# Layer 0's gate product on GpSimd instead of VectorE, in a four-layer graph network

## The chip, the cores and the metric

The kernel runs on one core of a Trainium2 chip. The metric is the device time of one execution in microseconds (us). Time before: the median of three runs is 3009.3 us (3008.72 to 3012.13).

The engines are named as in the profile: PE (TensorE, matmuls and transposes; PEld is its weight load), DVE (VectorE), ACT (ScalarE), POOL (GpSimd) and SP (SyncE, which here only starts DMAs). Each engine works off its own queue in order, and waits on semaphores for the others.

## The reference

Sixteen graphs (`B`) of 1024 nodes (`N`) with 128 features go through four layers, each followed by `x = layernorm(x + layer(x))`. Only layer 0 matters here, a gated attention over the adjacency matrix:

```python
h = x @ W_w.T + W_b
e = jnp.einsum('bjl,bkl->bjk', h @ A, h)
e = e + jnp.swapaxes(e, 1, 2)
att = jnp.where(adj > 0, e, -9e15)
att = jax.nn.softmax(att, axis=1) * adj
h_prime = jax.nn.relu(jnp.einsum('bij,bjk->bik', att, h))
coeff = jax.nn.sigmoid(jnp.concatenate([x, h_prime], axis=-1) @ gate_w.T + gate_b)
return coeff * x + (1.0 - coeff) * h_prime
...
x = _layernorm(x + _L0_gnn_ref(x, adj, ...), axis=-1)
```

`coeff` is one number for each node. With the residual, the sum to be normed is `(1 + coeff) * x + (1 - coeff) * h_prime`. The kernel takes the sigmoid from a tanh, so that `1 + coeff` is `0.5 * tanh + 1.5` (tile `cx`) and `1 - coeff` is `-0.5 * tanh + 0.5` (tile `co`).

Layer 1 is a graph convolution on a thinned adjacency matrix; a stage of its own does the thinning between layers 0 and 1. Layers 2 and 3 need a power of the nodes' degrees, among other things.

## The kernel before

`fast_kernel` does the work; `general_kernel` is a second path that runs only if a flag is set at the end, and it plays no part here. Nodes lie on 128 partitions in 8 tiles (`NT`), so that a graph's features are a tile of 128 x 8 x 128.

Layer 0 is written as three generators for a graph `b`, each cut into steps by `yield`:

- `before` loads x into `s.xn` (L916) and then, in eight steps, one block of 128 adjacency rows `an` (L920). ACT turns it into bf16 with the row sums (L922), DVE tests its values (L925, tile `chk`), PE transposes it (L929), and DVE writes the transposed 0/1 block as fp8 into `carry` (L930). In between come x transposed (L934), h (L938), the x part of the gate (L941), G (L945) and h in rows (L949). At the end POOL starts the write of the adjacency to DRAM (L951).
- `attention` does one column block in each of eight steps: the mask on ACT (L962), e on PE (helper line L723, tile `pmm`), the masked maximum on DVE (L965, which writes `em`), its negative (L967), the exponential on ACT (L969), reciprocal and scaled h on DVE (L971, L973), and the product on PE into `acc` (L976). There are two `em` buffers.
- `after` has three steps. The first takes relu (L982, tile `hpT`), the gate on PE (L774, L779), and `cx` and `co` on DVE (L985, L989, L990, with a tanh on ACT, L987). The second multiplies x by `cx` (L993), turns h' back with PE transposes (L758) and multiplies each half by `co` out of PSUM into `r` (L995, twice), then adds (L996). The third is the layernorm (`normed`: statistics L793 and L795, the power -1/2 on POOL L741 and L744, L798, and the scaling on ACT L800), and the write of the result, started by POOL (L999).

`in_turn` (L814) interleaves them: while graph b is in `attention`, graph b-1 is in `after` and graph b+1 in `before`, and each turn takes one step of each, in the order after, attention, before. For the last graph, `attention` runs with a step of `after` of graph 14 at every second step, and then `after` of graph 15 runs alone.

This written order is only a priority. When the kernel is built, each engine's queue gets its order from what counts as ready, so instructions of several steps, and of the stage that follows, stand between each other. The semaphores are set then too.

POOL does little in layer 0: for each graph the power in L744, and the start of the two writes L951 and L999. Once, POOL takes the power -1/2 of all 128 columns of degrees (L1177), after DVE has prepared them (L1176). These two lines are written after layer 0, in the thinning stage, and need only the row sums of all graphs.

Of the kernel before, what the change touches and what calls it, by code (L numbers as in the profile page):

```python
# [17 lines left out]
OP = mybir.AluOpType  # L18
# [621 lines left out]
def fast_kernel(ctx: ExitStack, tc: tile.TileContext, t: dict, out: bass.AP, flag: bass.AP):  # L640

    nc = tc.nc
# [43 lines left out]
    def nat(ap):  # L686
        return ap.rearrange("(t p) d -> p t d", p=P)
# [39 lines left out]
    def tiles3(ap):  # L727
        return ap.rearrange("p (t d) -> p t d", d=P)

    def per_row(v):  # L730

        return v[:, :, None].to_broadcast([P, NT, P])
# [20 lines left out]
    def turned(psum, src, tag="h"):  # L753

        for p, c, blocks in halves(psum, tag):
            for i, k in enumerate(blocks):
                s = src[:, k, :] if len(src.shape) == 3 else src[:, k * P:(k + 1) * P]
                nc.tensor.transpose(p[:, i * P:(i + 1) * P], s, identf)  # L758
            yield p, c, slice(blocks[0], blocks[-1] + 1)
# [8 lines left out]
    def gates(psum, out, *pairs):  # L768


        p = psum.tile([P, N // 4], F32, name="pq", tag="h")
        for i, (g, x) in enumerate(pairs):
            for q in range(4):
                nc.tensor.matmul(p[32 * q:32 * q + 32, :], g, x[:, q * N // 4:(q + 1) * N // 4], start=(i == 0),  # L774
                                 stop=(i == len(pairs) - 1), tile_position=(0, 32 * q))
        nc.scalar.copy(out, p)
        p = psum.tile([P, 2, P], F32, name="pg", tag="h")
        for t in range(2):
            nc.tensor.transpose(p[:, t, :], out[:, t * P:(t + 1) * P], identf)  # L779
        return p.rearrange("p t (q g) -> p q t g", q=4)  # L780

    def half_rows(v):

        return v[:, :, None].to_broadcast([P, 4, P])

    def normed(small, r, fine=False):

        for k in spans(fine):
            n = k.stop - k.start
            st = small.tile([P, NT, 6], F32, name="ln_st")  # L790
            mv = small.tile([P, NT, 2], F32, name="ln_mv")
            for i in range(n):
                nc.vector.bn_stats(st[:, i, :], r[:, k.start + i, :])  # L793
            for i in range(n):
                nc.vector.bn_aggr(mv[:, i, :], st[:, i, :])  # L795
            rstd = power_mhalf(small, mv[:, :n, 1], add=LN_EPS, name="ln_rstd")
            nb = small.tile([P, NT], F32, name="ln_nb")
            nc.vector.scalar_tensor_tensor(nb[:, :n], mv[:, :n, 0], -1.0, rstd, op0=OP.mult, op1=OP.mult)  # L798
            for i in range(n):
                nc.scalar.activation(r[:, k.start + i, :], r[:, k.start + i, :], AF.Identity,  # L800
                                     scale=rstd[:, i:i + 1], bias=nb[:, i:i + 1])
# [12 lines left out]
    def in_turn(before, attention, after, ahead=1, state=None):  # L814

        state = state or [Batch() for _ in range(B)]
        take_turns([before(state[b], b) for b in range(ahead)])
        for b in range(B - 1):  # L820
            streams = []
            if b:
                streams.append(after(state[b - 1], b - 1))
            streams.append(attention(state[b], b))
            if b + 1 >= ahead:
                streams.append(before(state[b + 1], b + 1))
            take_turns(streams)
        last, beside = attention(state[B - 1], B - 1), after(state[B - 2], B - 2)
        for i, _ in enumerate(last):
            if i % 2:  # L830
                next(beside, None)
        take_turns([beside, after(state[B - 1], B - 1)])
# [56 lines left out]
    with ExitStack() as ph:  # L889
# [89 lines left out]
        def after(s, b):  # L979

            hpT = work.tile([P, N], F32, name="hpT")
            nc.scalar.activation(hpT, s.acc, AF.Relu)  # L982
            pz = gates(ps_h, work.tile([P, NT, P], F32, name="r").rearrange("p t d -> p (t d)")[:, :N // 4], (gw[:, 1, :], hpT))
            co = small.tile([P, NT], F32, name="co")
            nc.vector.tensor_add(co.rearrange("p (q t) -> p q t", t=2), pz[:, :, :, 0],  # L985
                                 s.gx.rearrange("p (q t) -> p q t", t=2))
            nc.scalar.activation(co, co, AF.Tanh, scale=0.5, bias=gbh)  # L987
            cx = small.tile([P, NT], F32, name="cx")
            nc.vector.tensor_scalar(cx, co, 0.5, 1.5, op0=OP.mult, op1=OP.add)  # L989
            nc.vector.tensor_scalar(co, co, -0.5, 0.5, op0=OP.mult, op1=OP.add)  # L990
            yield
            r = work.tile([P, NT, P], F32, name="r")
            nc.vector.tensor_mul(s.xn, s.xn, per_row(cx))  # L993
            for p, c, k in turned(ps_h, hpT):
                nc.vector.tensor_mul(r[:, k, :], tiles3(p), half_rows(co[:, k]))  # L995
            nc.vector.tensor_add(s.xn, s.xn, r)  # L996
            yield
            normed(small, s.xn)
            nc.gpsimd.dma_start(nat(x1_d[b]), s.xn)  # L999
            yield  # L1000
# [723 lines left out]
```

## Time and profile before

| | |
|---|---|
| Median of three runs | 3009.3 us (3008.72 to 3012.13) |
| The profiled execution, as timed | 3009.7 us |
| Its span in the profile | 3007.9 us |
| Mean granted TensorE clock | 0.971 |
| L993 on DVE | 16 times, 1218 ns, starting from 92.3 to 723.2 us |
| L996 on DVE | 16 times, 1215 ns |
| L744 on POOL, 128 x 8 | 60 times, 1759 ns in the mean |
| L1177 on POOL, 128 x 128 | once, 20752 ns |

Times in a trace count from the start of the span. A line of the timeline gives the start, the duration, the engine, the line of the kernel, the operation, the tiles written and read, their shapes and a count; in square brackets stands the time that the engine was idle before it, and what ended the idle time. Consecutive DVE instructions overlap a little, so a duration of 1.22 us moves the next start by 1.13. A line of the view by stretches gives, for each engine, the busy time in us and the number of instructions. "PEclk" is the granted clock as a share of full speed.

### The profile page before, as it was taken

Reading aid. Unit: us, or ns where it says so; the run is one execution under the profiler, and the core shown is the slowest. Engines: PE = TensorE matmul, PEld = TensorE weight load, DVE = VectorE, ACT = ScalarE, POOL = GpSimd, SP = SyncE. Lnnn points to the kernel's source line nnn. Section 1 sums busy time; section 2 is a strip of 40 time slices with the busy share of each in tenths; the row PEclk is TensorE's granted clock in tenths of the full one; section 3 lists DMA queues with packets and bytes.
Section 4 is the critical chain, followed back from the end, with each engine's and each line's share of the span. In section 5 each row is a group of like instructions: output and inputs, shape, how many; then the busy total and the mean of one; then the engine's idle time right before and its main releaser. Section 6 shows DMA issues by size and latency. Waiting matters only on the chain.

```text
span 3007.9 us, 42998 instructions
## 1 busy us (share of the span) xinstructions
PE 2738.6 (91%) x15219; PEld 1719.6 (57%) x15282; DVE 2329.1 (77%) x5987; ACT 2028.3 (67%) x3475; POOL 324.1 (11%) x295
## 2 busy tenths in 40 slices
PE   7999999996999988999999987999999999999995
PEld 3444444443666566887788874455555555555554
DVE  6898899887999995776688785766777777777765
ACT  5777787774788877665555434766666676676763
POOL 0000000003000001211122231000010001000000
PEclk9999999998999999999999997999999999999998
DMA  4344444431000024223367692011111111111000
GB/s 157 133 161 153 135 140 161 148 126 36 2 2 2 2 102 143 99 99 127 127 234 250 227 342 84 36 56 58 63 69 61 64 70 66 56 57 57 22 15 23
DMA packets 124129, 297.98 MB, mean 99 GB/s; under 512 B 12672, under 2 KB 65664, under 8 KB 116736
## 3 DMA queue, kind: packets, MB, share of 16 engines
q1 hardware_dynamic: 103440, 211.65, 20.8%
q0 software_dynamic: 20464, 83.47, 7.4%
q8 instruction: 123, 2.02, 0.3%
q14 instruction: 102, 0.84, 0.1%
HBM read 211.04 MB, written 84.02 MB: 98 GB/s over the span
## 4 chain that ended last, share of the span: by engine, by line
PE 36%; DVE 23%; issue 21%; ACT 9%; DMA 6%; POOL 5%; SPq 0%; POOLq 0%; DVEq 0%; ACTq 0%
PE ph L1536 8%; PE acc L1293 6%; PE ph L765 5%; PE acc L1601 4%; DMA an<-in_adj 4%; PE pmm L723 3%; POOL ln_rstd L744 3%; DVE ln_st L793 3%; ACT xn L800 3%; PE ph L1397 3%; PE ph L758 3%; PE ph L1522 2%; DVE em L1587 2%; ACT em L969 2%; PE acc L976 2%
## 5 line engine op out<-in xcount | busy, mean ns | idle before, releaser
L723 PE MATMUL pmm<-G,hT 128*128 128x512 f32 x1024 | 505.9, 611 | 7.7 <-DVE mx L1587 7.2
L800 ACT ACTIVATE xn<-xn,ln_nb,ln_rstd 128x128 f32<-128x128 f32 x512 | 207.6, 481 | 115.2 <-DVE ln_nb L798 115.2
L723 PEld LDWEIGHTS pmm<-G,hT 128*128 128x128 f32 x1024 | 178.5, 193 | 175.5 <-issue 139.9
L976 PE MATMUL acc<-em,hs 128*128 128x512 f32 x512 | 243.3, 598 | 16.7 <-DVE hs L973 15.2
L1293 PE MATMUL acc<-a,lo 128*128 128x512 f32 x768 | 243.0, 400 | 15.2 <-DVE lo L1260 15.2
L744 POOL TENSOR_TENSOR ln_rstd<-ln_rstd,mhalf 128x8 f32<-128x8 f32 (+1 forms) x68 | 113.6, 1671 | 1329.1 <-DVE ln_rstd L741 608.8
L1601 PE MATMUL acc<-em,hs 128*128 128x512 f32 x512 | 249.3, 606 | 3.6 <-DVE hs L1598 1.9
L1293 PE MATMUL acc<-a,hi 128*128 128x512 f32 x768 | 244.1, 402 | 3.7 <-ACT hi L1259 3.5
L1140 ACT ACTIVATE q<-s,negc 128x512 f16<-128x512 f32 x256 | 170.5, 697 | 57.9 <-DVE negc L1119 22.3
L922 ACT ACTIVATE ab<-an 128x1024 bf16<-128x1024 f32 x128 | 134.5, 1052 | 105.9 <-DMA an<-in_adj 75.6
L1138 PE MATMUL s<-step,carry 128*128 128x384 bf16 (+3 forms) x1034 | 197.8, 302 | 7.5 <-DVE carry L1108 3.2
L1152 ACT ACTIVATE carry<-pc,negone 128x512 fp8e4<-128x512 f32 x256 | 166.8, 699 | 36.6 <-PE pc L1151 27.2
L965 DVE CUSTOM_DVE_ANT_0 em<-pmm,msk 128x1024 f32<-128x1024 f32 x128 | 155.9, 1218 | 30.0 <-PE acc L976 26.3
L1587 DVE CUSTOM_DVE_ANT_0 em<-pmm,msk 128x1024 f32<-128x1024 f32 x128 | 155.7, 1216 | 25.5 <-PE acc L1601 20.9
L1293 PEld LDWEIGHTS acc<-a,lo 128*128 128x128 f32 x768 | 143.9, 189 | 54.6 <-DVE lo L1260 21.2
L925 DVE SCALAR_TENSOR_TENSOR chk<-an 128x1024 fp8e4<-128x1024 f32 x128 | 156.4, 1222 | 14.8 <-DMA an<-in_adj 14.1
L1293 PEld LDWEIGHTS acc<-a,hi 128*128 128x128 f32 x768 | 142.9, 190 | 37.1 <-ACT hi L1259 4.0
L1582 ACT ACTIVATE msk<-A,nbig 128x1024 bf16<-128x1024 fp8e4 x128 | 145.8, 1140 | 26.7 <-DVE mx L1587 23.4
L930 DVE TENSOR_SCALAR carry<-pt 128x1024 fp8e4<-128x1024 bf16 x128 | 155.6, 1216 | 6.5 <-PE pt L929 6.5
L1397 PE MATMUL ph<-Wx,hT 128*128 128x128 f32 x768 | 152.3, 281 | 5.0 <-DVE l2WT L709 3.2
L969 ACT ACTIVATE em<-em,nmx 128x1024 f32<-128x1024 f32 x128 | 146.8, 1147 | 12.3 <-DVE nmx L967 11.9
L976 PEld LDWEIGHTS acc<-em,hs 128*128 128x128 f32 x512 | 90.7, 190 | 112.1 <-issue 86.8
(289 smaller groups left out, 6258.9 us busy)
## 6 DMA issues: line engine op xcount, KB each, us to landing
an<-in_adj SPq DMA_DIRECT2D x128, 512.0 KB, 4.1
adj_d<-carry POOLq DMA_DIRECT2D x16, 1024.0 KB, 4.9
A<-dil_d SPq DMA_DIRECT2D x16, 1024.0 KB, 6.8
rdeg<-rdeg_d SPq DMA_DIRECT2D x32, 512.0 KB, 4.3
ag_d<-ag POOLq DMA_DIRECT2D x32, 512.0 KB, 5.3
ag<-ag_d SPq DMA_DIRECT2D x32, 512.0 KB, 6.0
A<-adj_d SPq DMA_DIRECT2D x16, 1024.0 KB, 4.7
xn<-in_x SPq DMA_DIRECT2D x16, 512.0 KB, 4.0
```

The costliest lines, as they stand in the source:

```text
L723: nc.tensor.matmul(p[:, h * 512:(h + 1) * 512], lhsT, rhs[:, h * 512:(h + 1) * 512], start=True, stop=True)
L744: nc.gpsimd.tensor_tensor(r, r, mhalf[:, :n], op=OP.pow)
L800: nc.scalar.activation(r[:, k.start + i, :], r[:, k.start + i, :], AF.Identity, scale=rstd[:, i:i + 1], bias=nb[:, i:i + 1])
L969: nc.scalar.activation(em, em, AF.Exp, bias=nmx, accum_out=sm)
L976: nc.tensor.matmul(s.acc[:, c], hs, em[:, c], start=(jt == 0), stop=(jt == NT - 1))
L1138: nc.tensor.matmul(s[:, lo or 0:], y, twos if lo is None else step[:, :512 - lo], start=(j == 0), stop=(j == len(terms) - 1))
L1140: nc.scalar.activation(q[:, h * 512:(h + 1) * 512], s, AF.Abs, bias=st.negc[:, i:i + 1])
L1293: nc.tensor.matmul(acc, part[:, jt, :], pieces[h * NT // 2 + i][:, j, :], start=(jt == 0 and p == 0), stop=(jt == NT - 1 and p == 1))
L1397: nc.tensor.matmul(p[:, i * P:(i + 1) * P], x[:, j * P:(j + 1) * P], W, start=(n == 0), stop=(n == 1))
L1536: nc.tensor.matmul(p, part[:, jt, :], A[:, jt, c], start=(jt == 0 and i == 0), stop=(jt == NT - 1 and i == 1))
L1587: nc.vector.tensor_tensor_reduce(em, e, msk, 1.0, 0.0, op0=OP.add, op1=OP.max, accum_out=mx)
L1601: nc.tensor.matmul(s.acc[:, c], hs, em[:, c], start=(jt == 0), stop=(jt == NT - 1))
```

## The change

In the second step of layer 0's `after`, the product of x with `cx` is issued on GpSimd instead of VectorE. The operands, the result and the place in the written order stay as they are.

```diff
             r = work.tile([P, NT, P], F32, name="r")
-            nc.vector.tensor_mul(s.xn, s.xn, per_row(cx))
+            nc.gpsimd.tensor_tensor(s.xn, s.xn, per_row(cx), op=OP.mult)
             for p, c, k in turned(ps_h, hpT):
                 nc.vector.tensor_mul(r[:, k, :], tiles3(p), half_rows(co[:, k]))
             nc.vector.tensor_add(s.xn, s.xn, r)
```

The product now waits on POOL for `cx`, which DVE writes in L989, and the addition L996 on DVE waits for POOL.

## The prediction

> **What bounds the kernel now.** I read the page first, for which engine is full where; then stretches of layer 0; then single instructions around the moved one. The page's first part:
>
> ```profile
> PE 2738.6 (91%) x15219; PEld 1719.6 (57%) x15282; DVE 2329.1 (77%) x5987; ACT 2028.3 (67%) x3475; POOL 324.1 (11%) x295
> ```
>
> L993 runs only in layer 0, from 92.3 to 723.2 us, once for each of 16 batches, so only the first quarter of the span counts. One period of that loop, in the view of busy time by stretches:
>
> ```profile
> core 0: us, PE busy (x) PEld busy (x) DVE busy (x) ACT busy (x) POOL busy (x), PEclk, DMA share, GB/s
> ...
> 302.60:344.60 42.00, 39.28 (x180) 19.70 (x180) 37.60 (x91) 33.48 (x58) 3.17 (x3) 1.00 0.42 141
> ```
>
> A batch takes 42 us; PE is busy 39.3 of it, DVE 37.6, POOL 3.2. Two engines are nearly full and lean on each other, so an average can't say what 1.1 us of DVE is worth. The place of L993 can. The timeline of batch 8:
>
> ```profile
> 434.40 0.28 DVE L973 TENSOR_SCALAR hs<-hn,rs 128x128 f32<-128x128 f32 x1
> ...
> 434.74 1.98 PE L976 MATMUL acc<-em,hs 128*128 128x512 f32 x4 [0.54 <-DVE hs L973]
> ...
> 435.12 0.17 DVE L989 TENSOR_SCALAR cx<-co 128x8 f32<-128x8 f32 x1
> 435.33 0.17 DVE L990 TENSOR_SCALAR co<-co 128x8 f32<-128x8 f32 x1
> 435.41 1.22 DVE L993 TENSOR_TENSOR xn<-xn,cx 128x1024 f32<-128x1024 f32 x1
> 436.56 0.55 PE L929 MATMUL pt<-identb,ab 128*128 128x128 bf16 x7
> 436.76 1.22 DVE L965 CUSTOM_DVE_ANT_0 em<-pmm,msk 128x1024 f32<-128x1024 f32 x1
> ```
>
> L965 writes an em buffer that the acc matmuls (L976) must first have read; there are two. L993 begins at 435.41 and hands DVE on 1.13 us later, at about 436.54; L965 starts only at 436.76, 0.20 after PE's next work, L929, starts. So here DVE waits 0.2 us for PE even with L993 in place. What else DVE could do then isn't ready either: L930 needs those transposes of L929, L995 those of hpT, which come after.
>
> [...] No run here shows such a product on POOL. [...] L1176, with constants, takes 207 ns for 128 columns, L973, with a scalar per row, 278 ns.
>
> ```profile
> L1176 DVE TENSOR_SCALAR deg<-deg x1: 207/207/207, 685.2 to 685.2; 128x128 f32<-128x128 f32 x1
> ```
>
> [...] the granted clock is 1.00 to 724 us, and 0.50 at 728 to 732 with PE idle.
>
> **The change, part by part.** *Removed:* 16 L993 from DVE, each 1218 ns, 1.13 us from start to start. What each is worth is the start of L965 less the first moment it could start (L929's start plus the 0.20 above). For batches 1 to 13 that gives 0.30, 0.19, 0.12, 0.02, 0, 0.23, 0.11, 0, 0.19, 0.20, 0, 0.19, 0.01: 1.56 us together. From L965 on DVE runs without a gap to L996, so a start that doesn't move moves nothing. The other 13 x 1.13 - 1.56 = 13.1 us become idle DVE, hidden under acc matmuls of 1.9 us each. In batch 0, L965 and L990 stand ahead of L993; if L990 [...] must wait there for POOL, 1.1 us is lost as 1.13 is won; if not, up to 1.1 is won. I take 0.
>
> *Added:* 16 products on POOL. [...] bounds 1.2 (DVE's own time) and 4. POOL starts 0.14 us after cx (as L744 follows L741: end 316.93, start 317.07), so it ends 2.6 us after cx starts; L996, which now waits for it, comes at 7.2 in batches 1 to 13, at about 6.1 with L993 gone. Nothing waits, even at 4 us. Behind the product in POOL's queue stand L744 and the x_d write L999; POOL was idle 21 us before L744 (batch 8: 21.6), so both are untouched. L990 starts 0.2 after cx starts, ahead of POOL[...]. No DMA moves.
>
> *Moved, batch 14:* here POOL is not free. Its queue:
>
> ```profile
> 685.57 0.56 POOL L951 DMA_DIRECT2D adj_d<-carry  x1 [14.61 <-DVE deg L1176]
> 686.14 20.75 POOL L1177 TENSOR_TENSOR deg<-deg,mhalf 128x128 f32<-128x128 f32 x1
> 708.87 1.64 POOL L744 TENSOR_TENSOR ln_rstd<-ln_rstd,mhalf 128x8 f32<-128x8 f32 x1 [1.97 <-DVE ln_rstd L741]
> ```
>
> and DVE at that time:
>
> ```profile
> 699.43 0.17 DVE L989 TENSOR_SCALAR cx<-co 128x8 f32<-128x8 f32 x1
> ...
> 699.84 1.22 DVE L993 TENSOR_TENSOR xn<-xn,cx 128x1024 f32<-128x1024 f32 x1
> 700.97 1.28 DVE L995 TENSOR_TENSOR r<-ph,co 128x512 f32<-128x512 f32 x2
> 702.17 0.15 DVE L971 RECIPROCAL rs<-sm 128x1 f32<-128x1 f32 x1
> 702.29 1.23 DVE L996 TENSOR_TENSOR xn<-xn,r 128x1024 f32<-128x1024 f32 x1
> 703.43 0.28 DVE L973 TENSOR_SCALAR hs<-hn,rs 128x128 f32<-128x128 f32 x1
> 703.63 1.22 DVE L965 CUSTOM_DVE_ANT_0 em<-pmm,msk 128x1024 f32<-128x1024 f32 x1
> ```
>
> L1177, a power on 128 columns for the later layers, is written after layer 0, yet stands on POOL ahead of batch 14's L744: order is by readiness, and it is ready 13 us before this cx. So the product waits for 686.14 + 20.75 = 706.89, ends at 709.2, and L996 starts at 709.3 instead of 702.29: 7.0 us. Behind L996 in DVE's queue are hs L973 and L965 of attention in batch 15, and PE waits for both. PE's work before hs runs out at 704.4, so it idles some 6.3 us[...]. The acc matmul then takes about 3.6 instead of 1.88 and frees em for the next L965 at 714.3 instead of 706.22: 8.1 us. Bounds: 5.5 (L996 a few instructions later in the order) and 10.5 (product of 4 us). After that comes the same chain as before, to 723 us, with under 2 us of PE gaps to make some good.
>
> *Batch 15:* nothing else runs. Product 723.09 + 0.14 + 2.3 = 725.5, so L996 at 725.6 against 725.66: 0.1 won.
>
> **Sum:** -1.6 - 0.1 + 8.1 = +6.4 us on the profiled span of 3007.9, so 3014.3. The median of the runs is 3009.3, 1.4 above that span: **3015.7 us**.
>
> **The rivals.**
> *B, nothing is held:* the product gets ahead of L1177, or L996 is ordered so late on DVE that attention passes it. It decides if L996's place lies behind the work up to 709 us. For: the order is made again when the kernel is built, and a builder that knew of the 20.75 us would do so. Against: before, L798 was put at 318.77 ahead of L971, whose input was there from 316.1, and then waited 0.7 us for a power on 8 columns; the order seems to count POOL's powers as short. Time: -1.7, 3007.6. Not slower.
> *C, the freed DVE time is used:* DVE is on the chain that ended last, L993 among it with 4.9% of the stretch from 304 to 350 us. If the new order fills the gap, 14 x 1.13 = 15.8 is won, less 8.1: -7.7, 3001.6. Against: what DVE has next waits for PE.
> *D[...]:* if POOL's reading also shuts out L965 (msk from SBUF), L965 starts at cx + 2.6 instead of 1.4: 1.2 x 13 = 15.6 us, and with batch 14 less the small gains of L965, which then fall away, 15.6 + 8.1 = +23.7: 3033.
>
> **How the numbers follow.** A measurement of this kernel can tell about 0.2%, 6 us, from no change. The forecast (A) has 0.66, B 0.14, C 0.14, D 0.06. A's own range is 3012 to 3020 (batch 14 at 5.5 to 10.5, new orders worth some 2 us either way, gains of 0 to 2.7). The line of 3015.3 runs through A: 0.42 above, 0.24 below. B is 0.12 within and 0.02 faster, C faster, D slower. Slower 0.42 + 0.06 = 0.48, same 0.24 + 0.12 = 0.36, faster 0.14 + 0.02 = 0.16. The range leaves out D and nearly all of C: 3004.5 to 3020.
>
> **What would show it.** Right: POOL with 16 tensor_tensor of 128x1024 near 2.3 us; in batches 1 to 13 L965 within 0.3 us of its place after cx and a DVE gap of about 1.1 us before it, ended by PE acc; in batch 14 a DVE wait of some 8 us at L996 for POOL xn, just after L1177. Wrong: a period under 41.5 us in the loop (C), no long wait at L996 (B), or L965 lasting or starting 1 us later beside POOL (D).

## The result, and the profile after

The changed kernel takes 3024.7 us (median of six runs, 3016.1 to 3028.9), the kernel before 3010.1 us beside it (six runs, 3006.6 to 3013.4). The ratio is 1.0046, with a 95% interval of 1.0029 to 1.0062, which is 8.7 to 18.7 us. The forecast was +6.4 us and 3015.7 us, in a range that ended at 3020. So the sign was right, and the size was not.

The page's first part, of the kernel after (busy time, share of the span, instructions):

```profile
PE 2752.4 (91%) x15282; PEld 1721.3 (57%) x15282; DVE 2314.6 (76%) x5971; ACT 2030.5 (67%) x3475; POOL 354.8 (12%) x311
```

DVE lost 14.5 us of work and POOL gained 30.7 us. In the loop itself, the view of busy time for the same stretch as before, 302.6 to 344.6 us:

```profile
core 0: us, PE busy (x) PEld busy (x) DVE busy (x) ACT busy (x) POOL busy (x), PEclk, DMA share, GB/s
...
302.60:344.60 42.00, 39.55 (x179) 19.34 (x178) 36.63 (x89) 33.78 (x58) 5.10 (x4) 1.00 0.43 141
```

DVE is busy 36.6 instead of 37.6 us in it, and PE as before. Whether the period got shorter is read from the starts of `cx` (L989), one in each batch. The table gives three stretches between them, then the start of the thinning stage's first L1092, where layer 0 is over for DVE, and what is left of the span from there.

| kernel | cx 0 to cx 2 | cx 2 to cx 14 | cx 14 to cx 15 | L1092 starts | rest |
|---|---|---|---|---|---|
| before | 87.00 | 522.85 | 23.49 | 741.6 | 2266.3 |
| after | 90.99 | 522.84 | 31.49 | 751.9 | 2275.3 |
| after, profiled again (e5) | 91.36 | 523.22 | 32.73 | 752.4 | 2267.1 |

Three things are to be seen. The twelve periods in the middle took as long as before. Batch 14 costs 8.0 us. And the first two periods cost 4.0 us, which the prediction didn't have. With -0.5 us behind `cx` of batch 15 and a first `cx` that comes 1.2 us earlier (88.41 against 89.58 us; over all profiles it lies between 86.7 and 90.1), that makes 10.3 us at L1092.

**The steady periods.** The timeline of batch 8, after (start, duration, engine; in brackets the idle time before it and what ended it):

```profile
436.48 1.98 PE L976 MATMUL acc<-em,hs 128*128 128x512 f32 x4 [0.48 <-DVE hs L973]
...
436.87 0.17 DVE L989 TENSOR_SCALAR cx<-co 128x8 f32<-128x8 f32 x1
...
437.07 0.17 DVE L990 TENSOR_SCALAR co<-co 128x8 f32<-128x8 f32 x1
437.18 1.89 POOL L993 TENSOR_TENSOR xn<-xn,cx 128x1024 f32<-128x1024 f32 x1 [10.56 <-DVE cx L989]
...
438.30 0.55 PE L929 MATMUL pt<-identb,ab 128*128 128x128 bf16 x7
...
438.50 1.23 DVE L965 CUSTOM_DVE_ANT_0 em<-pmm,msk 128x1024 f32<-128x1024 f32 x1 [1.26 <-PE acc L976]
```

L965 still starts 0.20 us after L929, and 1.63 us after `cx` where it was 1.64 us before. In place of the product stands a gap of 1.26 us, ended by PE's `acc`. L965 itself lasts 1.23 us beside POOL's product, where it lasted 1.22 before, so POOL doesn't slow it. The view of DVE's waits, over the stretch from `cx` of batch 2 to that of batch 14, of the kernel before and then of the one after (total us, times, longest):

```profile
DVE em L965 <- PE acc L976: 20.7, 21, 1.5
```

```profile
DVE em L965 <- PE acc L976: 33.6, 37, 1.5
```

The wait grew by 12.9 us, which is nearly what leaves DVE there (12 products of 1.13 us, 13.6 us). That the freed time became waiting is shown by this. What sets the length of a period is not: on the chain that ended last, from batch 2 to batch 14, the largest entry is the loading of adjacency blocks (`an`), 18.1% before and 17.2% after, and no run varied it.

**Batch 14.** POOL's queue after the change:

```profile
688.96 20.75 POOL L1177 TENSOR_TENSOR deg<-deg,mhalf 128x128 f32<-128x128 f32 x1
709.69 1.89 POOL L993 TENSOR_TENSOR xn<-xn,cx 128x1024 f32<-128x1024 f32 x1
719.30 1.64 POOL L744 TENSOR_TENSOR ln_rstd<-ln_rstd,mhalf 128x8 f32<-128x8 f32 x1 [7.72 <-DVE nmx L967]
```

and DVE beside it:

```profile
702.24 0.17 DVE L989 TENSOR_SCALAR cx<-co 128x8 f32<-128x8 f32 x1
...
702.78 1.29 DVE L995 TENSOR_TENSOR r<-ph,co 128x512 f32<-128x512 f32 x2
711.61 1.23 DVE L996 TENSOR_TENSOR xn<-xn,r 128x1024 f32<-128x1024 f32 x1 [7.54 <-POOL xn L993]
```

The product stands behind the power, L996 behind the product, and the chain of waits from 702 to 734 us goes straight through them (start, us on the chain, what):

```profile
702.45 7.26 POOL deg L1177
709.71 1.88 POOL xn L993
711.59 0.02 issue
711.61 1.23 DVE xn L996
...
713.50 3.38 PE acc L976 x4
716.88 3.43 PE pmm L723 x8
```

PE idled 7.08 us before that `acc`, whose four matmuls then took 3.38 us, where four took 1.88 us before. The timeline of PE, before and after:

```profile
704.30 1.88 PE L976 MATMUL acc<-em,hs 128*128 128x512 f32 x4
```

```profile
713.50 3.38 PE L976 MATMUL acc<-em,hs 128*128 128x512 f32 x4 [7.08 <-DVE hs L973]
```

The mean granted clock after the change was 0.71 from 707 to 713 us and 0.59 from 713.5 to 717, where these four stand.

**The start of the loop.** DVE and POOL around `cx` of batch 0 and of batch 1, after:

```profile
88.72 1.90 POOL L993 TENSOR_TENSOR xn<-xn,cx 128x1024 f32<-128x1024 f32 x1 [9.79 <-PE acc L976]
...
135.62 1.89 POOL L993 TENSOR_TENSOR xn<-xn,cx 128x1024 f32<-128x1024 f32 x1 [13.23 <-PE ph L758]
```

```profile
89.89 0.76 DVE L990 TENSOR_SCALAR co<-co 128x8 f32<-128x8 f32 x1
90.56 1.21 DVE L930 TENSOR_SCALAR carry<-pt 128x1024 fp8e4<-128x1024 bf16 x1
...
135.51 0.17 DVE L990 TENSOR_SCALAR co<-co 128x8 f32<-128x8 f32 x1
135.59 2.00 DVE L973 TENSOR_SCALAR hs<-hn,rs 128x128 f32<-128x128 f32 x1
137.52 1.27 DVE L995 TENSOR_TENSOR r<-ph,co 128x512 f32<-128x512 f32 x2
```

L990 takes 0.76 us in batch 0 (0.17 in the others) and ends at 90.65, as POOL's product ends at 90.62. L973 takes 2.00 us in batch 1 (0.28 is its median) and ends at 137.59, just after POOL's product at 137.51. L973 takes the same, within 0.01 us, in all five profiles with this order (after, e1, e4, e5, e6), and so does L990 in three of them (after, e5, e6). In the kernel before, L973 did not stand there. Its DVE around `cx` of batch 1:

```profile
133.60 0.29 DVE L973 TENSOR_SCALAR hs<-hn,rs 128x128 f32<-128x128 f32 x1
...
134.00 0.17 DVE L990 TENSOR_SCALAR co<-co 128x8 f32<-128x8 f32 x1
134.08 1.22 DVE L993 TENSOR_TENSOR xn<-xn,cx 128x1024 f32<-128x1024 f32 x1
135.22 1.22 DVE L965 CUSTOM_DVE_ANT_0 em<-pmm,msk 128x1024 f32<-128x1024 f32 x1
```

The built order of batches 0 and 1 is another one after the change, though only one line was touched.

### The profile page after: what moved, and what is told of

Its sections match the earlier page's. It is cut to its first block, busy times and chain, and to the rows that moved or that the text cites. A ratio compares the mean times of both kernels' runs of the same rounds, so it can differ in the third digit from the quotient of the medians.

```text
span 3027.2 us, 43082 instructions
## 1 busy us (share of the span) xinstructions
PE 2752.4 (91%) x15282; PEld 1721.3 (57%) x15282; DVE 2314.6 (76%) x5971; ACT 2030.5 (67%) x3475; POOL 354.8 (12%) x311
## 4 chain that ended last, share of the span: by engine, by line
PE 43%; DVE 28%; issue 9%; ACT 8%; DMA 6%; POOL 5%; SPq 0%; POOLq 0%; DVEq 0%; ACTq 0%
PE ph L1536 8%; PE acc L1293 6%; PE ph L765 5%; PE pmm L723 4%; PE acc L1601 4%; DMA an<-in_adj 4%; POOL ln_rstd L744 3%; PE acc L976 3%; DVE ln_st L793 3%; ACT xn L800 3%; PE ph L758 3%; PE ph L1397 3%; PE s L1138 3%; DVE em L1587 2%; PE ph L1522 2%
## 5 line engine op out<-in xcount | busy, mean ns | idle before, releaser
L1138 PE MATMUL s<-step,carry 128*128 128x512 bf16 (+2 forms) x1088 | 212.3, 308 | 4.1 <-DVE carry L1108 3.2
L965 DVE CUSTOM_DVE_ANT_0 em<-pmm,msk 128x1024 f32<-128x1024 f32 x128 | 156.0, 1219 | 42.1 <-PE acc L976 37.9
L925 DVE SCALAR_TENSOR_TENSOR chk<-an 128x1024 fp8e4<-128x1024 f32 x128 | 156.3, 1221 | 17.4 <-DMA an<-in_adj 16.9
L962 ACT ACTIVATE msk<-carry,l0nbig 128x1024 bf16<-128x1024 fp8e4 x128 | 143.1, 1139 | 25.2 <-DVE mx L965 18.3
```

What stands on the lines that cost most here:

```text
L1138: nc.tensor.matmul(s[:, lo or 0:], y, twos if lo is None else step[:, :512 - lo], start=(j == 0), stop=(j == len(terms) - 1))
```

## The experiments

Theory: the time is lost in two places, in batch 14 (product behind the power) and in batches 0 and 1 (new order, and POOL's product holding up L990 and L973 of DVE), and what DVE is freed of in the middle is worth nothing. Rivals: the freed time is worth something that the two losses hide; the product costs time in every batch; the losses lie behind layer 0, where the profile after has 9 us more. The edits are against the changed kernel unless another is named.

| run | cx 0 to 2 | cx 2 to 14 | cx 14 to 15 | L1092 | time against before, 95% interval |
|---|---|---|---|---|---|
| e1, batch 14 on DVE | 90.59 | 526.18 | 23.50 | 747.9 | 1.0018 [1.0008, 1.0028] |
| e2, only batch 14 on POOL | 87.80 | 529.14 | 31.44 | 754.5 | 1.0031 [1.0018, 1.0043] |
| e3, no product | 88.00 | 521.63 | 22.74 | 738.9 | 1.0000 [0.9989, 1.0010] |
| e4, power in pieces | 90.29 | 524.48 | 36.99 | 759.4 | 1.0058 [1.0043, 1.0072] |
| e5, changed kernel again | 91.36 | 523.22 | 32.73 | 752.4 | 1.0044 [1.0029, 1.0058] |
| e6, batches 0 and 1 on POOL | 90.14 | 525.42 | 23.49 | 746.8 | 1.0020 [1.0010, 1.0030] |
| e7, batches 2 to 13 on POOL | 87.03 | 525.75 | 23.49 | 742.5 | 1.0003 [0.9993, 1.0013] |
| e8, r in hpT's place | 92.27 | 559.47 | 23.49 | 781.3 | 1.0153 [1.0136, 1.0170] |
| e9, e8 and a third em | 93.43 | 557.63 | 28.28 | 786.2 | 1.0156 [1.0139, 1.0173] |
| e10, e9 and batches 2 to 13 on POOL | 93.43 | 553.81 | 28.32 | 781.0 | 1.0119 [1.0102, 1.0136] |
| e11, batch 0 on POOL | 91.84 | 539.76 | 27.72 | 767.1 | 1.0079 [1.0059, 1.0098] |
| e12, batch 1 on POOL | 87.12 | 522.46 | 23.50 | 741.9 | 0.9999 [0.9989, 1.0009] |

How well one profile fixes these columns is seen in the table itself. In e2, batches 0 to 13 compute as before, and yet the middle took 529.1 us instead of 522.9: single periods of 45 to 46 us turn up in other batches from run to run. So a middle between 522 and 529 us tells nothing, while the outer two columns repeat within about 1.3 us. For the same reason L1092 came 3 to 5 us later in e1, e2 and e6 than was expected, and those figures test nothing.

### e1 and e2: batch 14 alone undone, and alone done

```
# e1
-nc.gpsimd.tensor_tensor(s.xn, s.xn, per_row(cx), op=OP.mult)
+(nc.gpsimd if b != 14 else nc.vector).tensor_tensor(s.xn, s.xn, per_row(cx), op=OP.mult)
# e2: b == 14 in place of b != 14
```

> The changed kernel, but batch 14's product stays on VectorE. The thinning stage's first comparison (L1092) starts at 741.6 us in the kernel before and at 751.9 in the changed one. Theory (the product of batch 14 is held behind the power L1177, and that is most of the loss in layer 0): L996 of batch 14 no longer waits for POOL, and L1092 starts 8 us earlier than in the changed kernel, at about 743 to 744, the 2 us left over coming from the start of the loop. Rival (the loss is spread over the batches by POOL's product beside DVE): L1092 stays above 749.

> Only batch 14's product is on GpSimd, the other fifteen stay on VectorE. Theory: the loss of batch 14 alone, a wait of about 7.5 us at its L996 and[...] 8 us in all: L1092 at about 749.5 to 750. Rival (spread over the batches): L1092 within 1 us of 741.6.

With batch 14 back on DVE the last interval is 23.50 us, as before the change; with batch 14 alone on POOL it is 31.44. In e2 the same wait stands at the same instruction:

```profile
704.92 1.29 DVE L995 TENSOR_TENSOR r<-ph,co 128x512 f32<-128x512 f32 x2
713.75 1.23 DVE L996 TENSOR_TENSOR xn<-xn,r 128x1024 f32<-128x1024 f32 x1 [7.54 <-POOL xn L993]
```

So batch 14 costs 8 us by itself. The timed losses, 0.18% without it and 0.31% with it alone, add up to 14.7 us, near the whole (12 to 15 us in e5 and in the first comparison), though each has an interval of 3 us or more to either side. What e1 still loses lies in its first two periods, 3.6 us longer than before.

### e3: the product left out

```
-nc.gpsimd.tensor_tensor(s.xn, s.xn, per_row(cx), op=OP.mult)
```

> The product of x with cx is left out altogether, on either engine, so x enters the sum unscaled. It shows what the freed time of VectorE is worth at most. Theory (L965 waits for the em buffer that the acc matmuls read): the 16 x 1.13 us that are freed turn into waits for PE acc, and in the batches 2 to 14 a period stays within 0.1 us of that before; L1092 at 739 to 741.6. Rival (VectorE bounds the loop): a period is 1.1 us shorter and L1092 starts near 725.

Here x enters the sum without its factor, and neither DVE nor POOL multiplies. The time is that of the kernel before: 1.0000, within 0.1% or 3 us, where 16 x 1.13 = 18 us of DVE work are gone. So the freed time is worth nothing that can be measured, whoever does the product. The gap before L965 is there just the same:

```profile
434.50 0.17 DVE L990 TENSOR_SCALAR co<-co 128x8 f32<-128x8 f32 x1
435.93 1.23 DVE L965 CUSTOM_DVE_ANT_0 em<-pmm,msk 128x1024 f32<-128x1024 f32 x1 [1.26 <-PE acc L976]
```

The run tells one more thing. In layer 0 its order on DVE, ACT and PE is that of the changed kernel, instruction for instruction; only POOL's products are missing. And its L973 of batch 1 is short:

```profile
135.29 0.17 DVE L990 TENSOR_SCALAR co<-co 128x8 f32<-128x8 f32 x1
135.38 0.28 DVE L973 TENSOR_SCALAR hs<-hn,rs 128x128 f32<-128x128 f32 x1
135.57 1.29 DVE L995 TENSOR_TENSOR r<-ph,co 128x512 f32<-128x512 f32 x2
```

Its first two periods take 88.00 us against 87.00 before and 90.99 after. So of the 4.0 us about 1.0 goes with the new order (itself within what two profiles can differ by, and less what leaving out two products may win), and 3.0 with POOL's product beside DVE. With the same order, the two timelines can be laid side by side from the first `cx` on: the changed kernel's DVE is 0.7 us later after L990 of batch 0 and 2.3 us later after L973 of batch 1. The lag stays until the end of the second period and becomes 3.0 us where L925 waits 0.71 us for a load of `an`, which it doesn't in e3.

### e4: the power in 16 pieces

```
-nc.gpsimd.tensor_tensor(dinv, deg, mhalf[:, 0:1].to_broadcast([P, BT]), op=OP.pow)
+[nc.gpsimd.tensor_tensor(dinv[:, i:i + NT], deg[:, i:i + NT], mhalf, op=OP.pow) for i in range(0, BT, NT)]
```

> The changed kernel, with the power of L1177 cut into 16 instructions of 8 columns, written in the same place. Theory: POOL takes batch 14's product between two pieces, so its L996 waits no more than one piece, 1.7 us, and L1092 starts at 743 to 745. Rival (the order on POOL is set when the kernel is built and puts all pieces ahead of the product): 16 pieces of 1.66 us hold it 26.6 us after the first has started, 6 us more than the one instruction, and L1092 starts at 757 or later.

All pieces were put ahead of the product (POOL's timeline; the 16 pieces are one row):

```profile
690.97 25.67 POOL L1177 TENSOR_TENSOR deg<-deg,mhalf 128x8 f32<-128x8 f32 x16
716.61 1.89 POOL L993 TENSOR_TENSOR xn<-xn,cx 128x1024 f32<-128x1024 f32 x1
```

They take 25.67 us together instead of 20.75, and the last interval grew from 31.5 to 37.0 us. Cutting the long instruction did not let the product in: the queue's order is fixed when the kernel is built, and there all pieces are ready first. This is the rival of the expectation, not its theory. It confirms the cause of the 8 us by making it larger.

### e5: the changed kernel once more

No edit.

> The changed kernel once more, for the part of the loss that lies after layer 0: from L1092 to the end of the span it took 2275.3 us in its profile and 2266.3 in that of the kernel before, though every queue has the same order there. Theory (a run's own variation, PE's clock and transfers): layer 0 ends within 0.5 us of 751.9 again, and the rest falls anywhere between 2264 and 2277. Rival (the later start of the rest costs something by itself): the rest is again 2275 within 2 us.

The rest of the span after L1092 is 2267.1 us here, against 2275.3 in the first profile of the same kernel and 2266.3 before the change. Over all 14 profiles it lies between 2263.1 and 2275.3, whatever layer 0 did. So the 9 us are not a repeatable effect of the change, and are not to be explained. The losses in the first two periods (91.36) and in batch 14 (32.73) are there again.

### e6 and e7: the start, and the middle

```
# e6
+(nc.gpsimd if b < 2 else nc.vector).tensor_tensor(s.xn, s.xn, per_row(cx), op=OP.mult)
# e7
+(nc.gpsimd if 1 < b < 14 else nc.vector).tensor_tensor(s.xn, s.xn, per_row(cx), op=OP.mult)
```

> Only the products of batches 0 and 1 are on GpSimd. Theory (POOL's product shuts out L990 of batch 0 for 0.6 us and L973 of batch 1 for 1.7 us, and the new order of the first period costs the rest): batch 2 starts its cx (L989) 2 to 3 us later than at 176.58, of which some 2 us are left at L1092: 743 to 744. Rival (the 2 us come from all batches alike): under 0.5 us.

> The products of batches 2 to 13 are on GpSimd, where POOL is free [...]; batches 0, 1, 14 and 15 stay on VectorE. Theory (a gap that ends with PE acc takes up the freed time): L1092 at 740.5 to 742, no difference that can be measured. Rival (twelve freed products of 1.13 us count): 13 us less, L1092 near 728.

The start alone costs 3.1 us in its own interval, and 0.20% of the time (3 to 9 us by the interval). The same long L973 is there, 2.00 us. The twelve batches in the middle cost and bring nothing: 1.0003, and a first interval as before (87.03). With that the product on POOL is harmless in the middle, as predicted, and the loss lies in batches 0 and 1, with their new order, and in batch 14.

### e8, e9 and e10: a third em buffer

```
# e8: r written into hpT's space, the gate's scratch moved, to make room
-r = work.tile([P, NT, P], F32, name="r")
+r = hpT.rearrange("p (t d) -> p t d", d=P)
-pz = gates(ps_h, work.tile([P, NT, P], F32, name="r").rearrange("p t d -> p (t d)")[:, :N // 4], (gw[:, 1, :], hpT))
+pz = gates(ps_h, early.tile([P, N], FP8, name="chk").bitcast(F32), (gw[:, 1, :], hpT))
# e9: e8, and
-em = work.tile([P, N], F32, name="em", bufs=2)
+em = work.tile([P, N], F32, name="em", bufs=3)
# e8 and e9 keep the product on DVE; e10: e9 with the product of batches 2 to 13 on POOL
```

> The kernel before, product on VectorE, with r written into hpT's space and the gate's scratch put into chk, which frees 4 KB a partition. The base for the two kernels with a third em buffer. Expected by both theories: no difference, the interval from the first cx to that of batch 14 within 3 us of the 609.85 before.

> As the base, with a third em buffer in layer 0, product on VectorE. Theory (VectorE's L965 waits for the buffer that the acc matmuls read, with PE behind it nearly full): some of the 22 us that L965 waited for PE acc go, and from batch 2 to 14 the loop gets 3 to 8 us shorter. Rival (the gap is PE's own: the pmm matmuls behind acc are late anyway): within 2 us of the base.

> As the one with a third em buffer, and the products of batches 2 to 13 on GpSimd. Theory: with L965 no longer held by the em buffer, the product's 1.13 us on VectorE stand on the path, so that the loop from batch 2 to 14 is shorter than with the third buffer alone by up to 12 x 1.13 = 13 us, at least by 4. Rival (something else, PE or the loads of an, takes the em buffer's place at once): within 2 us of it.

If L965 waits for the em buffer, a third one should take the wait away and let the freed DVE time count. Room for it was made by sharing other tiles, and this alone (e8) made the kernel 1.5% slower, where no difference was expected, with periods of some 46 us in another built order. So the three can only be read against each other. The third buffer does take the wait for `acc` away, and another comes in its place. What ended DVE's idle time before L965, e8 and then e9 (total us, times):

```profile
  PE acc L976: 23.9, 36
  PE pmm L723: 5.7, 11
```

```profile
  PE pmm L723: 21.4, 25
...
  PE acc L976: 0.9, 1
```

e9 is as slow as e8, and its middle only 1.8 us shorter, where the theory had 3 to 8. With the product on POOL on top (e10) the middle is 3.8 us shorter than in e9 and the time 10 us less (3050.5 against 3060.5 us), and their intervals don't quite touch. That could be a gain of the freed time where L965 has buffers enough; but 3.8 us is within what the middle varies by, the built orders differ, the granted clock was lower with three buffers (0.96 in the mean from 180 to 740 us, 1.00 in e8), and all three are slower than both kernels. It stays open.

### e11 and e12: batch 0 and batch 1 taken apart

```
# e11: b == 0, e12: b == 1
+(nc.gpsimd if b == 0 else nc.vector).tensor_tensor(s.xn, s.xn, per_row(cx), op=OP.mult)
```

> The product is on GpSimd in batch 0 alone; what VectorE does in batch 0 keeps the new order of the changed kernel, and from batch 1 on the product is VectorE's again. Theory (most of what the start of the loop loses is GpSimd's product of batch 1 shutting out hs, L973, which the new order puts right behind cx): the first period stays near 46.9 us (cx of batch 0 to cx of batch 1), the second falls from 44.1 to 44.5 to near 42.5, so the two together take 89.0 to 89.6 us instead of 91.0 to 91.4; L990 of batch 0 still takes some 0.7 us. Rival (the loss comes with the order of batch 0, whoever computes the product of batch 1): the two together stay at 90.5 or more. Timed: within 0.15% of the kernel before by the theory, 0.15 to 0.25% slower by the rival.

> The product is on GpSimd in batch 1 alone; batch 0 keeps VectorE's product and its old order, and in batch 1 L965 stands behind cx and co as before, with no instruction from SBUF to SBUF beside the product. Theory (the product costs only where an SBUF instruction of VectorE stands beside it, which takes the new order of the start): L965 keeps its 1.22 us, the first two periods take 87.0 to 88.0 us together as before, and the time is within 0.1% of the kernel before. Rival (a product on GpSimd costs at the start of the loop in any order): 89 us or more together, 0.1 to 0.2% slower.

e12 came out as the theory has it. The old order of batch 1 is kept, L973 stands ahead of `cx` and takes 0.29 us, and L965 takes its 1.22 us (timeline around the product):

```profile
134.13 0.29 DVE L973 TENSOR_SCALAR hs<-hn,rs 128x128 f32<-128x128 f32 x1
...
134.65 1.89 POOL L993 TENSOR_TENSOR xn<-xn,cx 128x1024 f32<-128x1024 f32 x1 [10.29 <-PE pg L779]
...
135.59 1.22 DVE L965 CUSTOM_DVE_ANT_0 em<-pmm,msk 128x1024 f32<-128x1024 f32 x1 [0.88 <-PE acc L976]
```

The time is 0.9999 of before. So POOL's product in batch 1 costs nothing in itself. In the changed kernel L973, which goes from SBUF to SBUF, stands beside it and takes 2.00 us; it stands there only in the order which batch 0's product brings.

e11 came out as neither account had it. Taking batch 0's product alone off DVE made the kernel 0.79% slower, more than taking all sixteen, although POOL multiplies only once. L990 of batch 0 was held up as in the changed kernel (0.87 us, 0.76 there). But the built order fell into another pattern for the whole loop: the twelve middle periods take 45.0 us each instead of 43.6. DVE's waits from `cx` of batch 2 to that of batch 14:

```profile
DVE rs L971 <- ACT em L969: 30.2, 25, 1.8
DVE em L965 <- PE acc L976: 17.5, 13, 2.7
DVE chk L925 <- DMA an<-in_adj: 15.4, 11, 1.6
```

Before the change the wait of L971 for ACT was 2.5 us there. The first two periods (91.84 us) thus say nothing on the share of L973, since they have this other order too; e3, with an unchanged order, stays the measure of it. What e11 shows is the size of the thing that was left out: an order that is made anew after one moved instruction can be 17 us worse over the twelve middle periods (25 us at L1092), though from 302 to 386 us no engine is busy for a larger share than before: PE 91% instead of 94%, DVE 85% instead of 90%.

## Why the prediction was wrong in size

*Batch 14: right.* It had L996 waiting for the product behind L1177, at +7.0 us, and 8.1 us for the loop. The trace has L996 9.37 us after `cx` instead of 2.86, so 6.5 us later (the product is 0.4 us shorter than the author's estimate of 2.3), PE idle 7.1 us (6.3 predicted), the four `acc` matmuls 3.38 us (3.6), and the interval 8.0 us longer. e1 and e2 show that it stands by itself, and rival B fell with it. The 3.6 was the author's estimate, for about half the clock: the profile before shows a granted clock of 0.50 from 728 to 732 us, with PE idle, and beside these four matmuls it was 0.59. That the sum came so near is in part luck: L996 came 0.5 us sooner than estimated, but PE's work ran out 0.8 us sooner too, counted from `cx`, and in e5 the same interval is 9.2 us longer. The gaps of PE that were to make some good add up to 2.3 us before, not under 2; none of it shows in the interval. And the granted clock before was 0.97 in the first 180 us, 1.00 only from there to 724; no term rests on either.

*Batches 1 to 13, the value of the freed time: right in the main thing, and the rest is noise.* The gap before L965 came as described, 0.8 to 1.3 us in batches 3 to 13, ended by PE's `acc`. The 1.56 us of small gains cannot be told: the middle moved by 0.01 us, in a column that varies by 6, so the close agreement is chance. e3 and e7 put the worth of the freed time at zero within about 0.1%. So rival C fell. Its sign, a period under 41.5 us, rested on a misreading: the 42 us that the prediction calls a batch are the stretch it chose, and the twelve periods take 43.6 us in the mean. No term of the sum uses it. Rival D fell as it was put: L965 keeps 1.22 to 1.23 us and its place. That L965 would keep both was the author's assumption, which no trace of the kernel before shows. But what D had in mind, POOL's product holding up work of DVE, is what cost time at the start, on other instructions (L990 0.76 us instead of 0.17, L973 2.00 instead of 0.28).

*Batch 0 and batch 1: wrong, and this is the step that failed.* The prediction put "I take 0" for batch 0, from a loss of 1.1 us against a gain of 1.13, and for batch 1 only its share of the small gains. What was measured is +4.0 us in the first two periods, and +3.1 to +4.4 in e1, e4, e5 and e6. Two assumptions were wrong in it. It took DVE's order around the product from the trace before (the range allowed 2 us either way for new orders, the sum nothing); but the built order of both batches changed, and e3 puts about 1.0 us on that. And it looked at L990 alone for a wait for POOL, of which no trace of the kernel before shows one: L973, a tensor_scalar of 128x128 from SBUF to SBUF, was set beside L1176 as the slower of the two (278 against 207 ns) and then left out, and it was not beside the product in the old order. In the new order it is, and it took 2.00 us instead of 0.28, 1.72 us more. The 0.59 us of L990 and the 1.72 us of L973 make 2.3 us lost on DVE, and none of it is made good before the end of the second period. Kernels with this same order up to batch 2, with POOL's product and without it (e3), differ by 3.0 us (after), 3.4 us (e5), 2.6 us (e1), 2.3 us (e4) and 2.1 us (e6), so the direct sum and the effect agree within what one profile can tell. L990 and L973 end within 0.1 us of the product's end (90.65 against 90.62, 137.59 against 137.51). L973 is listed 0.03 us before the product, at 135.59 against 135.62 us, but L990 ahead of it on DVE ends only at 135.68, after the product's start. The runs show that they are held while the product runs, and not without it (0.17 and 0.28 us in e3); by what is not shown.

*POOL's product: nearly right.* 1.89 us, 16 times, against 2.3, which was the author's estimate and which no trace of the kernel before shows; inside the bounds, and without effect except in batch 14.

*Batch 15: nearly right.* L996 waits 0.47 us for POOL and still comes 0.5 us earlier after `cx`, where 0.1 was predicted.

*The sum.* With the start at +4.0, the small gains at 0, batch 14 at +8.0 and batch 15 at -0.5, the same working gives +11.5 us or 1.0038, inside the measured 1.0029 to 1.0062. That is 3021 us, just above the range's end at 3020. The profiles themselves have +10.3 and +10.8 us at L1092 (after and e5), or +11.5 and +13.5 us when counted from the first `cx`. What the median has beyond that (14.6 us in the first comparison, 12.1 in e5) is within the interval; a small cost behind layer 0 is neither shown nor ruled out.

## What to carry to other kernels

Where a builder makes each queue's order, a moved instruction comes with a new order of its neighbours, and a term worked out on the old order needs a range for that: here it was worth nothing where DVE's order stayed (e12), about 1 us in e3 and 17 us over the middle of e11. An instruction given to GpSimd joins whatever its queue holds by then, work of later stages too, and a consumer in VectorE's queue passes that wait on to all behind it, as in batch 14, where L996 waited 7.54 us. Before moving work off an engine, leave the work out altogether and measure: e3 would have shown that there was nothing to win.

## What was not expected of the hardware

- A GpSimd product of 1.89 us held up a VectorE tensor_scalar with a scalar per row as it did one with constants: 2.00 us instead of 0.28 (L973, 128x128, SBUF to SBUF) in each of five profiles, and 0.76 instead of 0.17 us (L990, 128x8) in each of three. L965, which reads PSUM and SBUF, kept its 1.22 to 1.23 us beside the same product.
- The power on GpSimd takes 1.64 to 1.67 us for 8 columns in layer 0 and 20.75 us for 128; cut into 16 pieces of 8 it takes 25.67 us.
